# Attention with 64-column matmuls and two quantised convolutions: where the heads' half copies stand in ScalarE's queue, in what pieces an intermediate is read back, and in what order a projection's products are issued

## The chip, the cores and the metric

The kernel runs on one core of one Trainium2 chip. The metric is the device time of one execution in microseconds, as the median of several runs. The profile is that of one execution and is read beside the time of that same execution.

## The reference

There are 16 images of 128 channels and 32 x 32 pixels, in float32. Layer 0 is attention over the 1024 pixels with 4 heads of 128 channels each. Layer 1 is two 3 x 3 convolutions with quantised inputs and weights, each followed by a batch normalisation over all images.

```python
# layer 0
qkv = einsum('bchw,oc->bohw', x, w_qkv) + b_qkv           # 4 heads, q, k, v of 128 channels
scores = einsum('bnc,bcm->bnm', q, k) * c ** (-0.5)
attn = softmax(scores, axis=-1)
out = einsum('bnm,bmc->bnc', attn, v)                      # then heads side by side: 512 channels
x = einsum('bchw,oc->bohw', out, w_out) + b_out + x
# layer 1
identity = x
out = batchnorm(conv3x3(act_quant(x), weight_quant(w1)))   # act_quant: 16 levels in 0..1
out = batchnorm(conv3x3(act_quant(out), weight_quant(w2)))
x = out + identity
```

## The kernel before

**Attention.** The folded weights make one matrix per head out of the query and key weights, and one out of the value and output weights. Steps follow one another in one long list: 64 heads (image by image), four steps k = 0 to 3 per head. A step (`scores`) makes four score tiles of 128 keys by 512 queries. Each tile is a pair of products that write 64 output partitions each, the two *lanes*, and `halves` issues one on each lane. In the instruction stream of TensorE each float32 product stands as two matmuls. ScalarE exponentiates each tile (line 585) out of one of three PSUM banks `pss`, and VectorE forms the three further combinations that a seven-product scheme needs (`mix`, lines 570 to 574). One step later `attend` multiplies them with the turned input in seven products on alternating lanes and adds them up in four PSUM banks, `psa` 0 to 3, over the four steps of the head.

**The end of a head.** After the last `attend` of head g, in step `end`, ScalarE copies the four banks to SBUF. `evacuate` (line 625) takes banks 1 and 3 in the second half of step `end`. `evacuate_rest` (line 630) takes banks 0 and 2 in the next step, each behind one exponential of that step. `combine` then puts the quadrants together in three parts. Part 0 makes three copies between halves of the partitions (lines 641 to 643) and one sum on VectorE (L644). Part 1 copies `s3[BOTTOM]` from `y[TOP]` (L648) and adds (L649). Part 2 copies `sa[BOTTOM]` from `y[BOTTOM]` (L651) and adds twice (L653, L654). So L648 needs the sum L644, L649 needs L648, and L651 needs L649. Meanwhile the exponentials are summed by DMAs that accumulate (L595, issued by POOL, the first by SP). `sum_up` and `normalise` make the inverses, multiply (L721) and, at every second head, `mix` the result `z`.

**The projection.** When an image's four heads are done, `project_out` makes four banks, one at a time, out of `z` and the folded output weights `wb_sb` (L761). In banks 0 and 3 one of the two products has 512 columns and the other has 256, on the other lane. `gather_out` combines the four banks; a first convolution in six row filters follows in later steps (`rows_product`, `rows_output`), and its result is stored to `y1_dram`.

**What sets the order.** The calls are written down with `at(step, half, ...)`: half 0 runs between a step's scores and its attend, half 1 behind the attend. The compiler then orders each engine's queue by itself, earlier calls first among those that it holds ready, so an instruction written later can stand earlier in a queue. `tc.issue_after(ins)` holds an instruction behind another of the same engine. The list `stepped` holds the last step's four exponentials for that purpose. `product` ties TensorE's products into one chain with it; `project_out` does not use it. [...]

**The second convolution.** After the last head, `y1_dram` is read back in three pieces of 2, 3 and 10 images (L1174, queue of SP), and then the residual `res` (L1179). `quantize2` quantises an image: one ScalarE pass (L1189), one VectorE pass (L1190), and one on either engine (L1194 or L1196). Images 3, 5, 7, 9, 11 and 13 are convolved by row filters (`filtered_conv`, tiles `psf`), the others directly (`conv`, L282, tiles `psc`). In program order image 5 is quantised before image 4. At the end each image is scaled, the residual is added, and the result is stored.

Of the kernel before, what the change touches and what calls it, by code (L numbers as in the profile page):

```python
# [193 lines left out]
def fast_path(  # L194
# [18 lines left out]
    B, C, N = x.shape  # L213
# [28 lines left out]
    AWAY = range(0, B - 1)  # L242
    ys = [None if b in AWAY else keep.tile([P, N], F32, name=f"y{b}") for b in range(B)]
    pads = []
    for i in range(NPAD):
        t = padp.tile([P, H + 2, W + 2], BF16, name=f"pad{i}")
# [3 lines left out]
    def quantize(b, src, scale, bias, r0=0, r1=H):  # L250

        cut = slice(r0 * W, r1 * W)
        t = qtp.tile([P, (r1 - r0) * W], F32, tag="qt", name="qt")
        if b == B - 1 and scale == A_LEVELS and r1 == H:
            nc.vector.tensor_scalar(t, src[:, cut], scale, 0.0, ALU.mult, ALU.max)
        else:
            nc.scalar.activation(t, src[:, cut], AF.Relu, bias=bias, scale=scale)
        nc.vector.tensor_scalar(t, t, A_LEVELS, MAGIC, ALU.min, ALU.add)
        into = pads[b % NPAD][:, r0 + 1 : r1 + 1, 1 : W + 1]
        t = t.rearrange("p (h w) -> p h w", w=W)  # L260
        if b == B - 1:
            return nc.vector.tensor_scalar(into, t, MAGIC, FACTOR, ALU.subtract, ALU.mult)
        return nc.vector.tensor_scalar(into, t, MAGIC, None, ALU.subtract)
# [104 lines left out]
    with ExitStack() as ph:  # L368
# [20 lines left out]
        TOP, BOTTOM = slice(0, PH), slice(PH, P)  # L389
        LANES = (TOP, BOTTOM)  # L390
        NK = NCH // 2
        xt, us, xts, es, sides, avs, psa, accs, evs = {}, {}, {}, {}, {}, {}, {}, {}, {}
        zs, pjs, vlast = {}, {}, []
        exps, sums_added, attended, quantized, pe = [], [], [], [], []
        stepped = []
# [4 lines left out]
        def product(out_, lhsT, rhs, start=True, stop=True):  # L400

            with tc.issue_after(pe[0]) if pe else nullcontext():
                done = nc.tensor.matmul(out_, lhsT=lhsT, rhs=rhs, start=start, stop=stop)  # L403
            pe[:] = [done.ins]
            return done
# [50 lines left out]
        wb_sb = once.tile([P, 7, 2, PH], F32, name="wb_sb")  # L456
# [164 lines left out]

        def evacuate(g):
            evs[g] = [evp.tile([P, HALF], F32, tag=f"s{i}", name=f"ev_{g}_{i}") for i in range(4)]
            for i in (1, 3):
                nc.scalar.copy(evs[g][i], psa[g][i])  # L625

        def evacuate_rest(g):
            for n, i in enumerate((0, 2)):
                with tc.issue_after(stepped[n]):
                    nc.scalar.copy(evs[g][i], psa[g][i])  # L630
            psa.pop(g)

# [2 lines left out]
        def combine(g, part):  # L637
            sa, sb, s3, sd = evs[g]
            if part == 0:
                y = avs[g, "y"] = evp.tile([P, HALF], F32, tag="y", name=f"y_{g}")  # L640
                nc.scalar.copy(y[TOP], s3[BOTTOM])
                nc.scalar.copy(y[BOTTOM], sd[TOP])
                nc.scalar.copy(sd[TOP], sd[BOTTOM])
                nc.vector.tensor_tensor(y, sa, y, ALU.add)  # L644
                return
            y = avs[g, "y"]
            if part == 1:
                nc.scalar.copy(s3[BOTTOM], y[TOP])  # L648
                nc.vector.tensor_tensor(y, y, s3, ALU.add)  # L649
            elif part == 2:  # L650
                nc.scalar.copy(sa[BOTTOM], y[BOTTOM])  # L651
                avs[g] = avp.tile([P, N], F32, tag="av", name=f"av_{g}")
                nc.vector.tensor_tensor(avs[g][:, HALF:], y, sd, ALU.add)  # L653
                nc.vector.tensor_tensor(avs[g][:, 0:HALF], sa, sb, ALU.add)  # L654
                evs.pop(g), avs.pop((g, "y"))
# [93 lines left out]
        def project_out(b, bank):  # L749


            four = [
                [(0, A11, B11, W0), (1, S3, T3, W1)],
                [(1, A22, T4, W0), (0, A12, B21, W0)],
                [(1, S2, T2, W0), (0, S4, B22, W0)],
                [(1, S1, T1, W0), (0, S3, T3, W2)],
            ]
            ps = ps_m.tile([P, HALF], F32, tag="mm", name=f"pso_{b}_{bank}")
            for pair in range(2):
                for t, weight, head, cut in four[bank]:  # L760
                    nc.tensor.matmul(  # L761
                        ps[LANES[t], cut],
                        wb_sb[:, weight, pair],
                        zs[b, pair][:, head, cut],
                        start=(pair == 0),
                        stop=(pair == 1),
                    )
            if b not in pjs:
                names = ("sa", "sb", "s3", "sd", "y", "s2")
                pjs[b] = [pjp.tile([P, HALF], F32, tag=n, name=f"{n}_{b}") for n in names]  # L770
            sa, sb, s3, sd, y, s2 = pjs[b]
            if bank == 0:
                nc.scalar.copy(sa[TOP], ps[TOP])  # L773
                nc.scalar.copy(y[BOTTOM, W1], ps[BOTTOM, W1])
            elif bank == 1:
                nc.scalar.copy(sb, ps)
            elif bank == 2:
                nc.scalar.copy(s3[TOP], ps[TOP])
                nc.scalar.copy(s2[TOP], ps[BOTTOM])
            else:  # L780
                nc.scalar.copy(sd[BOTTOM], ps[BOTTOM])
                nc.scalar.copy(sd[TOP], ps[BOTTOM])
                nc.scalar.copy(y[BOTTOM, W2], ps[TOP, W2])
# [237 lines left out]
        def at(step, half, fn, *args):  # L1021

            later.setdefault(2 * step + half, []).append((fn, args))
# [8 lines left out]
        for hf in range(NHF):  # L1032
            warm_up(1)
            ps = ps_a.tile([P, HALF], F32, tag=f"a{2 + hf}", name=f"psu_0_{hf}")
# [16 lines left out]
        for g in range(LAST):  # L1051
            b, h = heads[g]

            end = (g + 1) * NK
            at(end + 1, 0, sum_up, g)
            at(end, 1, evacuate, g)
            at(end + 1, 0, evacuate_rest, g)
            at(end + 1, 0, combine, g, 0)
            at(end + 1, 1, combine, g, 1)
            at(end + 2, 0, combine, g, 2)  # L1060
            if b < B - 1:
                at(end + 4 - h % 2, 0, normalise, g)
            elif g < LAST - 1:
                at(end + 3, 0, normalise, g)
            else:
                at(end + 2, 1, normalise, g)
            at(max(g * NK + 1, 2), 0, project_u, g + 1, 0)
            at(max(g * NK + 2, 3), 0, project_u, g + 1, 1)
            if b < B - 1 and h == NH - 1:
                for bank, (step, half) in ((2, (5, 1)), (1, (6, 1)), (3, (7, 0)), (0, (7, 1))):  # L1070
                    at(end + step, half, project_out, b, bank)
                at(end + 8, 0, gather_out, b, 0)
                at(end + 8, 0, gather_out, b, 1)
                at(end + 9, 0, gather_out, b, 2)
            elif b == B - 1 and h < 2:
                for m, (step, half) in enumerate((((4, 1), (5, 1)), ((4, 1), (5, 0)))[h]):
                    at(end + step, half, project_plain, g, m)
            if h == NH - 1:
                at(end + 9, 1, lambda b: quantize(b, accs[b], A_LEVELS, 0.0), b)
                at(end + 10, 0, transform_rows, b)  # L1080
                at(end + 10, 1, sums_range, b)
                for i in range(len(PAIRS)):
                    at(end + 11 + (i + 1) // 2, (i + 1) % 2, rows_product, b, i)
                at(end + 13, 1, rows_output, b)
                at(end + 14, 0, first_statistics, b)
                if b + 2 < B:
                    at(end + 9, 1, load, b + 2, nc.scalar)
            if h == 2 and b + 1 < B:
                at(end - 2, 0, load_turned, b + 1, 0)
                at(end + 3, 1, turned_differences, b + 1, 0)  # L1090
                at(end + 3, 0, load_turned, b + 1, 1)
                at(end + 6, 1, turned_differences, b + 1, 1)
# [4 lines left out]
        for step in range(n_steps):  # L1097
            g, k = divmod(step, NK)
# [38 lines left out]
    with ExitStack() as ph:  # L1137
# [31 lines left out]


        scale1, bias1 = bn_params(0)
        for lo, hi in ((0, 2), (2, 5), (5, len(AWAY))):
            back = resp.tile([P, hi - lo, N], F32, name=f"back{lo}")
            nc.sync.dma_start(out=back, in_=y1d[lo:hi].rearrange("b c n -> c b n"))  # L1174
            for i in range(lo, hi):
                ys[AWAY.start + i] = back[:, i - lo]
# [55 lines left out]
        for r0, r1 in ((0, 10), (10, RPH + 2), (RPH + 2, H)):  # L1232
            first = quantize2(0, r0, r1)
# [23 lines left out]
        for b in range(B):  # L1257
            ends = parts.get(b, (0, N))
            for lo, hi in zip(ends, ends[1:]):
                y = ys[b][:, lo:hi]  # L1260
# [280 lines left out]
```

## Time and profile before

| what | value |
|---|---|
| median of 3 runs | 2025.08 us (2025.01 to 2025.44) |
| the profiled execution | 2024.81 us, span 2023.0 us |
| TensorE matmul / weight load | 1978.9 us (98%) / 967.3 us (48%) |
| VectorE | 1540.6 us (76%) |
| ScalarE | 1179.7 us (58%) |
| GpSimd | 182.6 us (9%) |
| mean granted TensorE clock | 0.992 |

A row of the page's groups reads: line, engine, operation, tile written and tiles read, shape, number; then busy time in us and the mean of one in ns; then the idle time of the engine just before these instructions and what ended most of it. A row of the waits reads: who waited for whom; then the sum in us, how often, and the longest. A row of a timeline reads: start, length, engine, line, operation and tiles, number of merged instructions, and in brackets the idle time before them with what ended it. A row of stretches gives, for each engine, its busy time and number of instructions, then the granted clock, the busy share of the DMA engines and what they moved in GB/s. Names such as `psa` leave out buffer numbers.

### The profile page before, as it was taken

How to read it: one execution, taken by the hardware profiler on the slowest of the kernel's cores; microseconds unless marked ns; L12 is line 12 of the kernel's file. 1: busy time of each engine (PE TensorE's matmuls, PEld its weight loads, DVE VectorE, ACT ScalarE, POOL GpSimd, SP SyncE). 2: the span in 40 equal slices, each digit the busy share in tenths (PEclk: the TensorE clock that was granted, in tenths of full speed). 3: DMA queues.
4: the chain of work that ended last, by engine and by line, in shares of the span. 5: the costliest groups of instructions: out<-in, count | busy, mean ns of one | idle time of the engine just before them, and what ended most of it. 6: DMA issues, size and time to landing. Idle time of an engine off the chain costs nothing.

```text
span 2023.0 us, 26071 instructions
## 1 busy us (share of the span) xinstructions
PE 1978.9 (98%) x9697; PEld 967.3 (48%) x9697; DVE 1540.6 (76%) x2703; ACT 1179.7 (58%) x2028; POOL 182.6 (9%) x218
## 2 busy tenths in 40 slices
PE   9999999999999999999999999999999999999983
PEld 4344544545454454545445454444544445454531
DVE  5786869778686876868787685878768597777887
ACT  4556556555655655565565556556565565656575
POOL 1110010100000000001000000100100000010020
PEclk9999999999999999999999999999999999999997
DMA  4333433433343433434334333433433343332184
GB/s 121 85 84 92 97 70 98 90 87 96 83 102 65 105 84 84 95 82 100 78 96 93 84 94 74 105 83 94 95 79 92 70 110 79 94 89 73 40 325 168
DMA packets 56216, 193.80 MB, mean 96 GB/s; under 512 B 6160, under 2 KB 6544, under 8 KB 56080
## 3 DMA queue, kind: packets, MB, share of 16 engines
q0 software_dynamic: 27216, 99.10, 25.7%
q1 hardware_dynamic: 25744, 83.18, 11.0%
q10 hardware_dynamic: 3120, 9.77, 1.5%
q8 instruction: 78, 1.28, 0.3%
q14 instruction: 58, 0.48, 0.1%
HBM read 35.27 MB, written 24.64 MB: 30 GB/s over the span
## 4 chain that ended last, share of the span: by engine, by line
PE 82%; DVE 12%; issue 3%; ACT 2%; DMA 1%; DVEq 0%; POOL 0%; ACTq 0%; POOLq 0%
PE pss L403 36%; PE psa L403 31%; PE pso L761 5%; PE psu L403 5%; DVE e L571 2%; PE psc L282 2%; PE psw L403 2%; DVE e L574 1%; ACT e L585 1%; DVE z L721 1%; DVE part L661 1%; DVE back L1267 1%; DVE e L570 1%; DVE side L689 1%; PE psf L1214 1%
## 5 line engine op out<-in xcount | busy, mean ns | idle before, releaser
L403 PE MATMUL pss<-u,x 128*64 128x512 f32 (+1 forms) x4128 | 1043.3, 590 | 4.4 <-ACT e L585 2.7
L403 PE MATMUL psa<-e,xt 128*64 128x512 f32 x3472 | 897.5, 592 | 0.0
L585 ACT ACTIVATE e<-pss 128x512 f32<-128x512 f32 x1008 | 591.6, 599 | 383.8 <-PE pss L403 375.9
L403 PEld LDWEIGHTS pss<-u,x 128*64 128x64 f32 x4128 | 430.5, 137 | 458.3 <-issue 346.7
L403 PEld LDWEIGHTS psa<-e,xt 128*64 128x64 f32 x3472 | 375.8, 137 | 377.0 <-issue 302.0
L570 DVE TENSOR_TENSOR e<-e 128x512 f32<-128x512 f32 x252 | 170.7, 678 | 309.9 <-ACT e L585 309.9
L571 DVE TENSOR_TENSOR e<-e 128x1024 f32<-128x1024 f32 x252 | 307.5, 1220 | 18.8 <-ACT e L585 13.7
L595 POOL DMA_DIRECT2D es<-e x189 | 163.0, 863 | 1695.0 <-DVE e L574 1157.2
L574 DVE TENSOR_TENSOR e<-e 128x512 f32<-128x512 f32 x252 | 173.1, 687 | 14.3 <-DVE e L571 0.9
L403 PE MATMUL psu<-x,at_sb 128*64 128x512 f32 x512 | 177.7, 595 | 0.0
L761 PE MATMUL pso<-z,wb_sb 128*64 128x512 f32 (+1 forms) x480 | 134.6, 540 | 0.0
L625 ACT COPY ev<-psa 128x512 f32<-128x512 f32 x126 | 70.8, 587 | 67.3 <-PE psa L403 66.8
L534 ACT ACTIVATE u<-psu,au_sb 128x512 f32<-128x512 f32 x127 | 87.3, 687 | 17.6 <-PE psu L403 15.6
L661 DVE TRANSPOSE_TENSOR_REDUCE part<-es 128x32 f32<-128x1024 f32 (+1 forms) x65 | 79.3, 1220 | 8.3 <-DMA es<-e 8.3
L403 PEld LDWEIGHTS psu<-x,at_sb 128*64 128x64 f32 x512 | 58.7, 138 | 56.4 <-issue 48.6
L648 ACT COPY ev<-y 64x512 f32<-64x512 f32 x63 | 38.9, 617 | 79.3 <-DVE y L644 79.3
L701 DVE STREAM_TRANSPOSE rb<-sums 128x1024 f32<-128x1024 f32 (+1 forms) x66 | 80.0, 1211 | 2.1
L721 DVE TENSOR_TENSOR z<-av,rb 128x512 f32<-128x512 f32 x120 | 78.2, 683 | 0.0
L761 PEld LDWEIGHTS pso<-z,wb_sb 128*64 128x64 f32 x480 | 53.3, 136 | 43.1 <-issue 41.4
L630 ACT COPY ev<-psa 128x512 f32<-128x512 f32 x126 | 72.8, 579 | 0.3 <-PE psa L403 0.3
L651 ACT COPY ev<-y 64x512 f32<-64x512 f32 x63 | 38.8, 616 | 58.7 <-DVE y L649 58.4
L789 DVE TENSOR_TENSOR y<-sa,s 64x512 f32<-64x512 f32 x15 | 10.2, 683 | 66.7 <-ACT sa L773 66.7
(193 smaller groups left out, 1384.7 us busy)
## 6 DMA issues: line engine op xcount, KB each, us to landing
es<-e POOLq DMA_DIRECT2D x189, 512.0 KB, 4.5
es<-e SPq DMA_DIRECT2D x63, 512.0 KB, 2.9
xt<-in_xturned_dram SPq DMA_DIRECT2D x32, 256.0 KB, 3.0
x_dram<-acc SPq DMA_DIRECT2D x16, 512.0 KB, 2.9
x<-in_x_dram ACTq DMA_DIRECT2D x15, 512.0 KB, 4.1
y_dram<-y SPq DMA_DIRECT2D x15, 512.0 KB, 2.6
res<-x_dram SPq DMA_DIRECT2D x1, 7680.0 KB, 38.6
back<-y_dram SPq DMA_DIRECT2D x1, 5120.0 KB, 20.9
```

Of the source, the lines that this page charges most:

```text
L403: done = nc.tensor.matmul(out_, lhsT=lhsT, rhs=rhs, start=start, stop=stop)
L534: copied = nc.scalar.activation(dst, ps, AF.Identity, bias=au_sb[:, h : h + 1])
L570: nc.vector.tensor_tensor(e[:, T3], e[:, B12], e[:, B22], ALU.add)
L571: nc.vector.tensor_tensor(e[:, T1 : T2 + 1 : T2 - T1], e[:, B12 : B11 + 1], e[:, B11 : T3 + 1 : T3 - B11], ALU.subtract)
L574: return nc.vector.tensor_tensor(e[:, T4], e[:, T2], e[:, B21], ALU.add)
L585: exps[:] = [nc.scalar.activation(e[:, 2 * c + 1 - m], ps, AF.Exp).ins]
L595: nc.gpsimd.dma_start(out=sides[g], in_=mine, accum_op=ALU.add)
L630: nc.scalar.copy(evs[g][i], psa[g][i])
L661: nc.vector.tensor_reduce(part, total.rearrange("p (k c) -> p k c", c=Q), AX.X, ALU.add, apply_transpose=True,)
L701: nc.vector.transpose(rb, rinv.unsqueeze(2).to_broadcast([P, n, Q]))
L721: nc.vector.tensor_tensor(z[:, 2 * (h % 2) + 1 - m], av[:, ts(m, HALF)], rb[:, ts(m, HALF)], ALU.mult)
L761: nc.tensor.matmul(ps[LANES[t], cut], wb_sb[:, weight, pair], zs[b, pair][:, head, cut], start=(pair == 0), stop=(pair == 1),)
```

## The change

In `evacuate`, bank 2 is copied along with banks 1 and 3, and only bank 0 is left for `evacuate_rest`, behind the first exponential of the step. Part 1 of `combine` moves from the second half of step `end + 1` to the first half of `end + 2`, where part 2 already is (in the last image it stays), and the two half copies L648 and L651 are held behind the second and the fourth exponential. `normalise` of every second head moves by half a step. `project_out` issues its products through `product`, in an order written out: in banks 1 and 2 as before, in banks 0 and 3 the first, the second, the second and the first again. The read back of 10 images is cut into one of 4 and one of 6.

```diff
         def evacuate(g):
             evs[g] = [...]
-            for i in (1, 3):
+            for i in (1, 3, 2):
                 nc.scalar.copy(evs[g][i], psa[g][i])

         def evacuate_rest(g):
-            for n, i in enumerate((0, 2)):
-                with tc.issue_after(stepped[n]):
-                    nc.scalar.copy(evs[g][i], psa[g][i])
-            psa.pop(g)
+            with tc.issue_after(stepped[0]):
+                nc.scalar.copy(evs[g][0], psa.pop(g)[0])
...
             if part == 1:
-                nc.scalar.copy(s3[BOTTOM], y[TOP])
+                with tc.issue_after(stepped[1]):
+                    nc.scalar.copy(s3[BOTTOM], y[TOP])
                 nc.vector.tensor_tensor(y, y, s3, ALU.add)
             elif part == 2:
-                nc.scalar.copy(sa[BOTTOM], y[BOTTOM])
+                with tc.issue_after(stepped[3]):
+                    nc.scalar.copy(sa[BOTTOM], y[BOTTOM])
...
-            for pair in range(2):
-                for t, weight, head, cut in four[bank]:
-                    nc.tensor.matmul(
-                        ps[LANES[t], cut],
-                        wb_sb[:, weight, pair],
-                        zs[b, pair][:, head, cut],
-                        start=(pair == 0),
-                        stop=(pair == 1),
-                    )
+            first, second = four[bank]
+            order = [(*first, 0), (*second, 0), (*second, 1), (*first, 1)]
+            if bank in (1, 2):
+                order = [(*first, 0), (*second, 0), (*first, 1), (*second, 1)]
+            for t, weight, head, cut, pair in order:
+                product(
+                    ps[LANES[t], cut],
+                    wb_sb[:, weight, pair],
+                    zs[b, pair][:, head, cut],
+                    start=(pair == 0),
+                    stop=(pair == 1),
+                )
...
-            at(end + 1, 1, combine, g, 1)
+            at(*((end + 1, 1) if b == B - 1 else (end + 2, 0)), combine, g, 1)
             at(end + 2, 0, combine, g, 2)
             if b < B - 1:
-                at(end + 4 - h % 2, 0, normalise, g)
+                at(end + 4 - h % 2, h % 2, normalise, g)
...
-        for lo, hi in ((0, 2), (2, 5), (5, len(AWAY))):
+        for lo, hi in ((0, 2), (2, 5), (5, 9), (9, len(AWAY))):
```

## The prediction

> **What bounds the kernel now.** I read the page first, then the waits, then the instruction timelines of one batch and of the second convolution.
>
> ```profile
> span 2023.0 us, 26071 instructions
> ...
> PE 1978.9 (98%) x9697; PEld 967.3 (48%) x9697; DVE 1540.6 (76%) x2703; ACT 1179.7 (58%) x2028; POOL 182.6 (9%) x218
> ...
> PEclk9999999999999999999999999999999999999997
> ```
>
> TensorE is busy nearly to the end at full clock, so only time in which it does less than it could counts. "Busy" hides half of that. In the attention part the products are 64 columns wide and run on two lanes. In the trace's list of matmuls each lane starts one 512-column matmul every 0.43 us, and a moment with one lane idle still reads as busy. So I listed the start of every matmul, took 0.427 us for 512 columns, half for 256, and summed what each lane waited beyond that. From 8 to 1876 us the average of the two lanes is idle 23.2 us, although the union shows only 4.4. Some 18 us of it stands in four places that recur or come once: head 0 of a batch, third step, 5.7 us over 15 batches; head 3, third step, 4.5 us over 14; projection bank 3, 2.5 us over 15 (0.33 us of one lane each); the weight folds and constants of the first batch, about 5, which the change does not touch. The waits name the first two:
>
> ```profile
> ACT ev L648 <- DVE y L644: 79.3, 63, 3.1
> ...
> ACT ev L651 <- DVE y L649: 58.4, 60, 1.6
> ...
> PEld pss L403 <- ACT e L585: 48.0, 112, 1.9
> ```
>
> ScalarE sits in two half copies of `combine` until VectorE has added, and score matmuls wait for exponentials. ScalarE's timeline in head 0 of batch 6 shows the order:
>
> ```profile
> 728.66 0.69 ACT L534 ACTIVATE u<-psu,au_sb 128x512 f32<-128x512 f32 x1
> 731.08 0.62 ACT L648 COPY ev<-y 64x512 f32<-64x512 f32 x1 [1.73 <-DVE y L644]
> 732.48 0.62 ACT L651 COPY ev<-y 64x512 f32<-64x512 f32 x1 [0.78 <-DVE y L649]
> 733.12 1.57 ACT L585 ACTIVATE e<-pss 128x512 f32<-128x512 f32 x3
> ```
>
> The third step's score matmuls start at 730.67; two products take 0.86, so its first exponential could have begun near 731.7. It begins at 733.12, behind both copies. With three score banks the fourth tile needs the first exponential's bank: the lanes stop for 0.29 and 0.53 us at 733.77.
>
> After attention the largest single hole, in TensorE's timeline and ScalarE's:
>
> ```profile
> 1943.23 4.64 ACT L1189 ACTIVATE steps<-back,bias,scale 128x1024 bf16<-128x1024 f32 x4 [2.26 <-DVE half L1228]
> ...
> 1949.65 5.50 PE L282 MATMUL psc<-pad,wq 128*128 128x512 bf16 x18 [7.33 <-DVE pad L1194]
> ```
>
> The releaser "half" ended long before; what really ended is the third read back:
>
> ```profile
> 1921.80 1.65 SPq L1174 DMA_DIRECT2D back<-y_dram  x2
> ...
> back<-y_dram SPq DMA_DIRECT2D x1, 5120.0 KB, 20.9
> ```
>
> Its issue is at 1922.3, plus 20.9 gives 1943.2. Image 5, whose quantising stands first in ScalarE's queue, is in that piece; image 4, which TensorE needs next, arrived in the piece before but queues behind it.
>
> **What the Trainium skill says.** "PSUM — Partial Sum Buffer", Engine vs sequencer instructions: ScalarE's queue is strictly first in, first out. The trace agrees: exponentials at 733.12 follow the copy's end at 733.10. "TensorE: Matmul & The Clock Gate", Part 1: over 3.4 us of idleness halve the clock. It agrees: after the 7.33 us hole 18 matmuls take 5.50 us, against 3.97 in the chain of waits later. "DMA: Bandwidth & Descriptors", Queues, rings and completion order: one queue's descriptors are consumed in ring order. The landings agree roughly: the three pieces and `res` land in the order of issue at 1924.1, 1930.1, 1943.2 and 1962.1.
>
> **The change, part by part.** No matmul, DVE operation or byte is added; one DMA is.
>
> *Combine's copies, a step later.* L648 goes from the half step before the third step's scores to behind their second exponential, L651 behind the fourth. Both still cost 0.62 us, 126 copies in all, in ScalarE time that is 42% idle. The first exponential is then no longer behind a DVE wait. If L648 itself has to wait, exponentials three and four queue behind it; L644 ended at 731.04 in head 0 and at 821.8 in head 3, before the second exponential would end (1.02 us after the scores' start for the first tile, 0.86 for the second, 0.60 of its own: 733.1 and 824.4), so there is nothing to wait for. Behind L651 stand one `u` copy and the next step's exponentials, 3.4 us away. The DVE adds (0.68 us each) follow their copies; `mix` may shift by one add, while the attend that needs it starts 2.4 us after it ended (739.1 against 741.5). Gain: 5.7 + 4.5 = 10.2 us at most, nothing at least. I take 8.5, leaving a sixth for heads where another ScalarE copy comes first.
>
> *Normalise of odd heads half a step later.* Only DVE operations move, no DMA and nothing on POOL or SP. `z` was finished at 739.7 and its projection begins at 754 or later: cost nothing, cover 14 us.
>
> *Evacuation 1, 3, 2 before, only 0 between exponentials.* A third copy of 0.58 us moves ahead of the next step's first exponential, and one of the two in between goes. That work sum is zero. Those places hold two half copies of 0.62 as fillers; if one moves back, the exponential stays at 724.93, where it is. Its latest harmless start: scores begin at 723.18, the fourth tile is needed 2.57 later, less 0.60, so 725.15, a margin of 0.22. Value zero; bounds −1 (a slightly earlier release) and the third rival below.
>
> *Projections' order.* Bank 3 went lane 1 (512), 0 (256), 1 (512), 0 (256):
>
> ```profile
> 772.55 0.59 PE L761 MATMUL pso<-z,wb_sb 128*64 128x256 f32 x2
> 772.87 0.59 PE L403 MATMUL pss<-u,x 128*64 128x512 f32 x1
> 773.30 1.02 PE L761 MATMUL pso<-z,wb_sb 128*64 128x512 f32 x4
> ```
>
> The first narrow pair starts at 772.55 and occupies its lane for 0.43 us; the second could not start before 773.31, since a wide product stood between them. With 1, 0, 0, 1 both narrow products run together. Gain 0.33 / 2 x 15 = 2.5 us. Bank 0 had no gap and needs none; banks 1 and 2 keep their order. Bound below: 0. I take 2.2. The chain that now holds these products in order is the order they had.
>
> *Read back in four.* Images 5 to 8 become a piece of 2.10 MB. From 1930.1 to 1943.2 5.24 MB came, 0.40 MB/us, so they land at 1930.1 + 5.2 = 1935.3, 7.8 us earlier. SP issues one more DMA, some 0.4 us, ahead of `res`, which lands at 1962 and is needed at 1995: nothing. Image 4's quantising then fits into ScalarE's idle 1.3 us gaps of 1935 to 1941, and TensorE could go on at 1942.3: 7.3 us of hole and 1.5 of slow clock, 8.9 at most. VectorE is next:
>
> ```profile
> 1935.00:1943.00 8.00, 7.32 (x34) 2.95 (x31) 4.33 (x8) 2.35 (x4) 2.21 (x2) 1.00 1.03 424
> 1943.00:1949.00 6.00, 0.00 (x0) 0.00 (x0) 5.79 (x9) 4.64 (x4) 2.67 (x2) 0.72 1.01 418
> 1949.00:1955.00 6.00, 5.35 (x19) 2.10 (x20) 4.39 (x8) 4.98 (x6) 2.67 (x2) 0.71 1.03 424
> 1955.00:1992.00 37.00, 37.00 (x178) 17.09 (x176) 33.85 (x58) 24.33 (x32) 6.84 (x6) 1.00 0.19 76
> ```
>
> From 1935 to 1992 its busy column sums to 48.4 us of 57. Eight of idleness can go, and I leave 2 in which it waits for inputs: gain 6.5, bounds 0 (pieces interleave and land together) and 8.9. Images 9 to 14 still land near 1943; ScalarE has 10 us of work before it asks for image 9.
>
> **Sum.** The profiled execution took 2024.8 us, 1.8 more than its span and 0.3 less than the median of the runs. 8.5 + 2.2 + 6.5 = 17.2, so 2007.6, and with the 0.3 about 2008.
>
> **Rivals.**
> Forecast, 0.62: as above, 2003 to 2014 from the bounds.
> *Only the read back and the lanes pay*, 0.19: the bank copies moved ahead of the exponential take what the half copies give back, some 0.15 us a head. 2025.1 − 8.7 = 2016; with the read back alone 2019. For it: the margin of 0.22. Against: filler copies can yield.
> *Slower*, 0.15: at the evacuation ScalarE takes three bank copies and both half copies before the first exponential, which then starts at 725.5. That exponential, its neighbours and bank 0's copy, now behind the first one and possibly behind the third, all come late; the next head's attend, whose first product writes bank 0, starts at 726.6 and would find it copied 0.6 to 1.0 us late. 62 heads x 0.8 = 50, less the 17: about 2058. It decides from 17.2 / 62 = 0.28 us of lane stop per head. Against it: the half copies were put before the exponential only where it was not ready.
> *Nothing moves*, 0.04: the copies stand in the same places in the queue as before and the pieces land together; 2025.
>
> Two tenths of a per cent, 4 us, is about what a measurement of this kernel tells from no change. The first two cases and part of the fourth give faster 0.81, same 0.04, slower 0.15. The range 2002 to 2022 holds the first two cases, some 0.81.
>
> **What would show it.** Right: L648 and L651 between exponentials with hardly any idle before them; the wait of score weight loads for exponentials well under 48 us; no 0.33 us gap between bank 3's narrow products; the hole before the fifth image's convolution (7.33) under 1.5 us and 18 matmuls there in about 4 us. Wrong: an idle time of attend products for L630, first exponentials starting over 1.7 us after their scores, ScalarE still waiting for a read back near the same place, or a new hole at image 9.

## The result and the profile after

The changed kernel takes 2002.36 us (median of 4 runs, 2000.92 to 2002.61) against 2025.05 us before (4 runs, 2024.70 to 2025.44). The ratio is 0.9886, with a 95% interval of 0.9869 to 0.9904. It is faster, by 22.7 us where 17.2 were forecast, and lies just below the 2003 to 2014 that the prediction's bounds gave for its own case. The profiled execution took 2000.92 us, 23.9 less than that of before. It can be cut at the first `psc` matmul of the second convolution, which stands at 1919.5 before and at 1903.5 after. Of the 23.9 us, 15.9 lie ahead of it, in the attention part, and 8.0 behind it.

In the file of the changed kernel the two half copies are L647 and L651, the sum that L651 waits for is L648, `quantize2` is L1192 to L1199, and the read back is L1177. The page's first rows:

```profile
span 1999.1 us, 26134 instructions
...
PE 1966.2 (98%) x9697; PEld 982.7 (49%) x9697; DVE 1536.5 (77%) x2703; ACT 1181.8 (59%) x2028; POOL 182.4 (9%) x218
```

TensorE's share is 98% as before. The share cannot show the gain, because a moment with one idle lane counts as busy. From the waits (who waited for whom, sum in us, times, longest):

```profile
ACT ev L651 <- DVE y L648: 31.5, 17, 2.2
...
PEld pss L403 <- ACT e L585: 22.1, 81, 0.4
...
ACT ev L647 <- DVE y L642: 1.0, 1, 1.0
```

Score weight loads wait 22.1 us for exponentials instead of 48.0, and never longer than 0.4. The copy L647 waits once in the whole kernel. The copy L651 still waits 1.9 to 2.2 us in one head of 15 images, but it stands behind the last exponential of its step, and the lanes do not stop there. ScalarE's timeline in head 0 of batch 6, the place shown before:

```profile
726.20 0.60 ACT L585 ACTIVATE e<-pss 128x512 f32<-128x512 f32 x1 [2.79 <-PE pss L403]
727.06 0.60 ACT L585 ACTIVATE e<-pss 128x512 f32<-128x512 f32 x1 [0.26 <-PE pss L403]
727.68 0.62 ACT L647 COPY ev<-y 64x512 f32<-64x512 f32 x1
728.32 1.09 ACT L585 ACTIVATE e<-pss 128x512 f32<-128x512 f32 x2
729.43 0.62 ACT L651 COPY ev<-y 64x512 f32<-64x512 f32 x1
```

The first exponential now waits for its scores and for nothing else, and both copies run between exponentials without idle time before them. For the read back, SP's queue and then TensorE's timeline:

```profile
1905.85 2.31 SPq L1177 DMA_DIRECT2D back<-y_dram  x3
```

After the first piece three more are issued in a row instead of two. TensorE's work in the second convolution:

```profile
1924.88 1.49 PE L1217 MATMUL psf<-rows,wq 128*128 128x512 bf16 x6
1926.20 4.13 PE L282 MATMUL psc<-pad,wq 128*128 128x512 bf16 x18
...
1934.00 4.13 PE L282 MATMUL psc<-pad,wq 128*128 128x512 bf16 x18 [1.02 <-ACT pad L1199]
...
1941.03 4.13 PE L282 MATMUL psc<-pad,wq 128*128 128x512 bf16 x18 [0.26 <-ACT pad L1199]
```

The hole of 7.33 us is gone: image 4's 18 matmuls follow directly and take 4.13 us. What is left are holes of 1.02 and 0.26 us before images 6 and 8.

The idle time of the two lanes was summed again from the list of matmul starts, as in the prediction, here from 8 us to the first `psc` matmul, in us as the average of the two lanes. The three columns in the middle are experiments described below. Each column is one profiled execution, and an idle time beside a change of step can fall to either side, so a tenth means little:

| place | before | order alone | half copies alone | bank copies alone | after |
|---|---|---|---|---|---|
| head 0, third step | 6.5 | 9.7 | 0.0 | 0.4 | 0.0 |
| head 3, third step | 4.0 | 2.1 | 0.0 | 0.9 | 0.0 |
| projections | 2.9 | 0.2 | 0.5 | 0.8 | 0.0 |
| first image | 6.8 | 6.8 | 5.2 | 6.1 | 5.1 |
| all else | 5.0 | 6.0 | 4.3 | 5.9 | 5.0 |
| sum | 25.2 | 24.7 | 9.9 | 14.1 | 10.1 |

The sum falls by 15.1 us, which is nearly the 15.9 that attention became shorter.

### The profile page after: what moved, and what is told of

Same layout as the page of the kernel before. It is cut to its first block, busy times and chain, and to the rows that moved or that the text cites. A ratio compares the mean times of both kernels' runs of the same rounds, so it can differ in the third digit from the quotient of the medians.

```text
span 1999.1 us, 26134 instructions
## 1 busy us (share of the span) xinstructions
PE 1966.2 (98%) x9697; PEld 982.7 (49%) x9697; DVE 1536.5 (77%) x2703; ACT 1181.8 (59%) x2028; POOL 182.4 (9%) x218
## 4 chain that ended last, share of the span: by engine, by line
PE 97%; DVE 1%; ACT 1%; issue 0%; DVEq 0%; POOL 0%; ACTq 0%; POOLq 0%
PE pss L403 44%; PE psa L403 38%; PE psu L403 6%; PE pso L403 5%; PE psw L403 2%; PE psc L282 2%; DVE back L1270 1%; PE psf L1217 1%; PE unread L403 0%; ACT steps L1192 0%; PE psv L403 0%; ACT back L1267 0%; ACT pad L1199 0%; PE ps_a L403 0%; DVE late L292 0%
## 5 line engine op out<-in xcount | busy, mean ns | idle before, releaser
L403 PE MATMUL pss<-u,x 128*64 128x512 f32 (+1 forms) x4128 | 1032.4, 589 | 0.0
L403 PEld LDWEIGHTS pss<-u,x 128*64 128x64 f32 x4128 | 438.5, 137 | 434.9 <-issue 399.1
L403 PEld LDWEIGHTS psa<-e,xt 128*64 128x64 f32 x3472 | 379.9, 137 | 371.1 <-issue 352.0
L403 PE MATMUL psu<-x,at_sb 128*64 128x512 f32 x512 | 183.4, 592 | 0.0
L625 ACT COPY ev<-psa 128x512 f32<-128x512 f32 x189 | 99.2, 593 | 63.1 <-PE psa L403 61.7
L792 DVE TENSOR_TENSOR y<-sa,s 64x512 f32<-64x512 f32 x15 | 10.2, 683 | 66.4 <-ACT sa L776 66.4
L651 ACT COPY ev<-y 64x512 f32<-64x512 f32 x63 | 38.8, 616 | 32.7 <-DVE y L648 31.5
L403 PE MATMUL psw<-rows,filters 128*64 128x256 bf16 x540 | 57.5, 277 | 0.0
L403 PEld LDWEIGHTS <-filters 128*64 128x64 bf16 x540 | 44.8, 109 | 24.0 <-issue 18.6
```

## The experiments

The theory was that of the prediction: three of the five edits pay, each for a stop of its own. The rivals were that some edit does another's work, and that the three bank copies ahead of the exponential cost something. Where a kernel is described as "before plus" or "changed kernel less", nothing else differs.

### The read back alone

Before plus one line:

```diff
-        for lo, hi in ((0, 2), (2, 5), (5, len(AWAY))):
+        for lo, hi in ((0, 2), (2, 5), (5, 9), (9, len(AWAY))):
```

> The kernel before with the read back in four pieces and nothing else. Theory (the whole hole goes, and the slow clock behind it): 8.0 us less than before, convolution of image 4 starting right behind image 3's. Rival, as predicted (VectorE leaves 2 us): 6.5 us less. Rival (pieces land together): no change, hole of 7 us still there.

Measured: 2017.11 us against 2024.95, ratio 0.9961 (0.9947 to 0.9974), so 7.8 us. Images 5 to 8 landed at 1935.5, where the prediction had 1935.3. TensorE's timeline of this kernel:

```profile
1941.83 4.13 PE L282 MATMUL psc<-pad,wq 128*128 128x512 bf16 x18
...
1949.63 4.13 PE L282 MATMUL psc<-pad,wq 128*128 128x512 bf16 x18 [1.02 <-ACT pad L1196]
```

The hole before image 4 is gone and 1.02 us comes back one image later, as in the changed kernel. This edit is separate from the others.

### Images 4 and 5 quantised in the order of need, three pieces kept

```diff
-            if b + 2 < B and b + 2 not in FILTERED:
+            if b + 2 < B and b + 2 not in FILTERED and b != 2:
                 quantize2(b + 2)
+            if b == 1:
+                quantize2(4)
```

> The kernel before with three pieces as they were, but image 4 quantised before image 5 in program order. Theory (half of the hole is queue order: image 4 was there since 1930 and only stood behind image 5; image 5 still lands at 1943 and its row filters are ready 5 us later): convolution of image 4 follows without a hole, a new one of 2 to 3 us stands before image 5's, 4 to 6 us less than before. Rival (only the landing counts): no change, the same hole of 7 us one image later.

Measured: 2021.22 us against 2025.33, ratio 0.9980 (0.9971 to 0.9988), so 4.1 us:

```profile
1941.94 4.13 PE L282 MATMUL psc<-pad,wq 128*128 128x512 bf16 x18
...
1952.20 4.13 PE L282 MATMUL psc<-pad,wq 128*128 128x512 bf16 x18 [1.40 <-ACT pad L1196]
```

Image 4 never needed the big piece; it only queued behind image 5. With the order alone its hole goes too, but image 5 itself still waits for 5.24 MB, and holes of 1.29, 0.45 and 1.40 us follow. So the smaller piece is worth 7.8 us, and the order of the queue with the big piece about half of that.

### The projections' order alone

Before plus the new `project_out`.

> The kernel before with the projection's products chained in the written order and nothing else. Theory (one narrow product no longer waits for a wide one on the other lane): 2.5 to 2.9 us less, lane gaps at the projections gone. Rival (the gap is only moved to the next product of the lane): no change, another gap of 0.3 us behind bank 3.

Measured: 2024.34 us against 2024.95, ratio 0.9993 (0.9985 to 1.0001): not told apart from nothing. The theory fell. The gaps of the projections are gone (2.9 to 0.2 in the table), but head 0's third step took some 3 us more (6.5 to 9.7), while head 3's took 1.9 less. The waits of this kernel show that the cause of these stops is still there:

```profile
ACT ev L648 <- DVE y L644: 76.3, 49, 3.0
...
PEld pss L403 <- ACT e L585: 45.2, 115, 2.1
```

In most images the list of starts shows an exchange: one lane no longer loses 0.33 us at bank 3, and in the next head 0 the two lanes stop for 0.29 and 0.75 us instead of 0.29 and 0.53. In two images the stops there are longer, of 1.0 and 1.5 and of 1.3 and 1.8 us, which makes up over half of the 3 us. The profiled execution was the slowest of the 13 (2025.47), and three others took 2022.0 to 2022.6. Whether these had no such long stops is not shown.

### The half copies alone

```diff
             if part == 1:
-                nc.scalar.copy(s3[BOTTOM], y[TOP])
+                with tc.issue_after(stepped[1]):
+                    nc.scalar.copy(s3[BOTTOM], y[TOP])
...
             elif part == 2:
-                nc.scalar.copy(sa[BOTTOM], y[BOTTOM])
+                with tc.issue_after(stepped[3]):
+                    nc.scalar.copy(sa[BOTTOM], y[BOTTOM])
...
-            at(end + 1, 1, combine, g, 1)
+            at(*((end + 1, 1) if b == B - 1 else (end + 2, 0)), combine, g, 1)
```

> The kernel before with the two half copies (L648, L651) moved alone; evacuation 1, 3 then 0, 2 and normalise stay. Theory (the half copies ahead of the first exponential are the whole cause): 12 us less, as with all the head parts together. Rival (bank 2's copy between the exponentials delays the sum that L648 waits for, so that the third exponential waits behind it): 4 to 8 us less, with idle time of ScalarE before L648.

Measured: 2010.61 us against 2024.95, ratio 0.9925 (0.9912 to 0.9939), so 14.3 us, more than the 12 of the theory. Both third steps stand at zero in the table, and the projections fell to 0.5 although their order is the old one. TensorE's timeline at a third bank shows why:

```profile
762.69 4.00 PE L403 MATMUL pss<-u,x 128*64 128x512 f32 x16
766.13 1.42 PE L763 MATMUL pso<-z,wb_sb 128*64 128x256 f32 x6
```

Four narrow matmuls and two wide ones stand merged in one row. By the list of starts the narrow ones begin at 766.13, 766.34, 766.56 and 766.80, without the gap of 0.33 us, and the first wide one at 766.53. So the narrow lane is 0.40 us ahead here, where it was 0.76 ahead in the kernel before (772.55 and 773.30). In both kernels, and in all 15 images, the second narrow pair begins just behind the first wide matmul and never ahead of it. As a narrow pair takes 0.43 us, a lead of 0.76 leaves a gap of 0.33, and a lead of 0.40 leaves none.

The lead goes with the stops. Here a gap is left in the first image alone (0.28 us), where some stops remain. In the kernel with the bank copies alone, described below, gaps of 0.31 to 0.37 us stand in four images of 15: in the first, and in three that follow a stop of 0.3 us or more; the other eleven have no stop of over 0.1 us ahead of them. That it is the unevenness of a stop that puts one lane ahead is inferred: the two lanes stop for 0.29 and 0.53 us in head 0 of the kernel before, which is 0.24 of the 0.35 us between the two leads, but the trace does not name the lanes.

In the profiled execution attention ended 16.1 us earlier, but 2.0 of that was lost behind it, 1.5 of them in one place:

```profile
1933.56 7.00 PE L282 MATMUL psc<-pad,wq 128*128 128x512 bf16 x18 [7.33 <-DVE pad L1196]
```

The hole is the same 7.33 us, but the matmuls after it take 7.00 us and not 5.50. The stretches of this kernel (length; busy time and number for TensorE, its weight loads, VectorE, ScalarE, GpSimd; then clock, DMA share, GB/s) show the clock still at half from 1936 to 1938 and for a part of the next 2 us:

```profile
1936.00:1938.00 2.00, 2.00 (x6) 0.73 (x5) 1.56 (x2) 1.58 (x3) 1.82 (x2) 0.50 1.03 424
1938.00:1940.00 2.00, 2.00 (x8) 0.69 (x6) 1.23 (x3) 2.00 (x3) 0.00 (x0) 0.62 1.03 426
1940.00:1942.00 2.00, 2.00 (x11) 0.89 (x10) 0.71 (x2) 1.76 (x4) 0.00 (x0) 1.00 1.01 418
```

By the starts of the matmuls it was back at full 6.0 us after 1933.56. In the kernel before it was back 2.9 us after the hole's end at 1949.65:

```profile
1952.50:1954.50 2.00, 2.00 (x10) 0.88 (x9) 1.56 (x3) 2.00 (x3) 1.42 (x2) 1.00 1.03 424
```

### All the head edits

Half copies, bank copies and `normalise` together, with old projections and three pieces.

> The kernel before with everything that concerns the heads (evacuation 1, 3, 2 then 0; half copies behind the second and fourth exponential a step later; normalise of odd heads half a step later), without the projection's order and the read back. Theory (lane waits for exponentials go whole, the small ones behind them too): 12 to 13 us less, and the three single parts add up to the 22.7 of the whole change. Rival, as predicted (a sixth stays): 8.5 us less; then the parts would not add up, and some 5 us came from their acting together.

Measured: 2009.70 us against 2024.95, ratio 0.9923 (0.9910 to 0.9937), so 15.3 us. Next to the half copies alone (14.3, intervals overlapping) the other head edits add nothing that can be told. Attention ends at 1903.4 in both.

### The changed kernel less the new order

> The changed kernel with the projection's old products (no chain, both pairs in the same order). Theory (bank 3's gap was the offset between two lanes that the heads' uneven stops had left; without those stops the lanes run in step): within 0.7 us of the changed kernel, gaps at the projections under 0.6 us in all 15 images. Rival, as predicted (the order of a wide and a narrow product makes the gap): 2.2 to 2.9 us more than the changed kernel, 0.33 us in each image.

Measured: 2001.54 us, ratio 0.9882 (0.9867 to 0.9898), against 0.9886 for the changed kernel. The order is worth nothing that can be told there either: with the stops gone there is a gap in the first image alone for it to close.

### The changed kernel less the half copies

L648 and L651 back at their old place.

> The changed kernel with the two half copies back where they stood (a half step earlier, behind no exponential); banks 1, 3, 2, normalise, projection order and read back stay. Theory (these two copies are nearly all of the heads' gain): 13 to 15 us more than the changed kernel, with a lane wait of some 9 us in the third step of head 0. Rival (copying bank 2 early brings the sums forward, so that the copies no longer wait): 3 us or less more.

Measured: 2005.69 us against 2025.33, ratio 0.9903 (0.9888 to 0.9918), only some 3.3 us over the changed kernel, a quarter of what the half copies gain by themselves. The theory (13 to 15) fell. So another of the edits does nearly the same work; the next kernel has it alone.

### The bank copies alone

```diff
-            for i in (1, 3):
+            for i in (1, 3, 2):
...
-            for n, i in enumerate((0, 2)):
-                with tc.issue_after(stepped[n]):
-                    nc.scalar.copy(evs[g][i], psa[g][i])
-            psa.pop(g)
+            with tc.issue_after(stepped[0]):
+                nc.scalar.copy(evs[g][0], psa.pop(g)[0])
```

> The kernel before with the bank copies alone changed: 1, 3 and 2 together, 0 behind the first exponential; the half copies, normalise, projections and read back are as before. Theory: copying bank 2 one step-half earlier by itself lets the part-0 copies and VectorE's sum end about 8 us sooner, so that both half copies are done before the third step's scores need the exponential. Then it gains nearly what all four head edits gained without the half copies (about 11 to 12 us): 2013 to 2014.5, and TensorE's wait of score weights for exponentials falls from 48 to about 25 us. Rival: it needs normalise's later half-step to get the sum early; then it gains under 5 us, over 2020. Second rival: with the three bank copies ahead of the exponential and the half copies there too it is slower than 2025.

Measured: 2013.20 us against 2024.98, ratio 0.9941 (0.9928 to 0.9955), so 11.8 us, as the theory said. ScalarE's timeline in head 0 of batch 6, then the sum of part 0 on VectorE, then a row of the waits (line numbers two lower: the half copies are L646 and L649):

```profile
724.35 0.62 ACT L646 COPY ev<-y 64x512 f32<-64x512 f32 x1
726.45 0.61 ACT L649 COPY ev<-y 64x512 f32<-64x512 f32 x1 [1.48 <-DVE y L647]
727.12 0.60 ACT L585 ACTIVATE e<-pss 128x512 f32<-128x512 f32 x1
```

```profile
722.87 0.68 DVE L642 TENSOR_TENSOR y<-ev,y 128x512 f32<-128x512 f32 x1
```

```profile
PEld pss L403 <- ACT e L585: 24.7, 78, 1.3
```

Both half copies still stand ahead of the exponential, and the second still waits, but both are done in time. Counted from the first exponential of the step before (719.91 here, 724.93 before), the sum starts 3.0 us later here and 5.4 later in the kernel before: bank 2 is copied sooner, so is what is copied out of it, and VectorE takes the sum 2.5 us sooner in its queue. The expectation's "8 us" compared absolute times of two executions and was wrong by the 5 us that this kernel had gained up to there. Against the half copies, 4 us of lane time are left: in heads of batch 15 and in head 3 of batches 10 and 12, where the copies are late all the same, and in the first image.

### The changed kernel less the bank copies

> The changed kernel with the old bank copies (1 and 3 together, 0 and 2 behind the first and second exponential). Theory: bank copies and half copies remove the same wait, so with the half copies moved this is worth nothing: 2001 to 2003, within 1 us of the changed kernel. Rival: bank 2's earlier copy has a share of its own (attend of the next head finds its bank earlier): 2 to 4 us slower, and TensorE's attend products wait for the copy.

Measured: 2000.82 us, ratio 0.9879 (0.9863 to 0.9894). Beside the half copies the bank copies are worth nothing that can be told; the median is 1.5 us below that of the changed kernel, and the ranges of the runs overlap.

### The changed kernel less the move of normalise

> The changed kernel with normalise of every second head at its old half step. Theory: z is finished some 14 us before its projection in either place, so nothing: within 0.7 us of the changed kernel at about 2002. Rival: normalise in the old place stands in VectorE's queue ahead of a sum or a mix that the next attend needs: 2 us or more slower, with attend products waiting for mix.

Measured: 2001.83 us, ratio 0.9884 (0.9869 to 0.9899). Worth nothing that can be told, as predicted.

### Two edits of five

Before plus the half copies' move and the four pieces.

> Two of the five edits: the half copies behind the second and fourth exponential, and the read back in four pieces. Bank copies, normalise and the projections' order are as before. Theory: gains of the two add, 14.3 and 7.8 us, so 2003.0 (2002 to 2004), within 1.5 us of the changed kernel at 2002. Rival: bank copies, normalise and order together are worth over 3 us beside them: over 2005.

Measured: 2001.55 us against 2024.98, ratio 0.9882 (0.9867 to 0.9898), so 23.4 us: all of the changed kernel's gain. Its wait of score weight loads is that of the changed kernel too:

```profile
PEld pss L403 <- ACT e L585: 21.6, 81, 0.4
```

This kernel and the three that take away the order, the bank copies or `normalise` lie between 2000.8 and 2001.8. None can be told from the changed kernel, so no better version was shown, only simpler ones.

### The predicted slower case, brought about

The changed kernel with the three half copies of part 0 written at the evacuation, so that they stand ahead of the next step's exponentials. Part 0 keeps its sum alone:

```diff
         def evacuate(g):
...
             for i in (1, 3, 2):
                 nc.scalar.copy(evs[g][i], psa[g][i])
+            sa, sb, s3, sd = evs[g]
+            y = avs[g, "y"] = evp.tile([P, HALF], F32, tag="y", name=f"y_{g}")
+            nc.scalar.copy(y[TOP], s3[BOTTOM])
+            nc.scalar.copy(y[BOTTOM], sd[TOP])
+            nc.scalar.copy(sd[TOP], sd[BOTTOM])
```

> The changed kernel with the three half copies of combine's first part written in front of the step's scores, so that three bank copies and two or three half copies stand before its first exponential, and bank 0's copy behind the third. Nothing is added. This is the rival that the prediction priced. Theory (the fourth score tile and the first attend product stop the lanes once the exponential is later than 1.97 us after its scores): 0.8 to 1.7 us in each of 62 heads, 50 to 105 us more than the changed kernel. Rival (three banks of scores and a later catch-up swallow it): under 10 us more.

Measured: 2045.39 us against 2025.33, ratio 1.0099 (1.0083 to 1.0114). That is 43.0 us over the changed kernel, or 0.69 for each of 62 heads. ScalarE's timeline and the waits:

```profile
733.64 0.62 ACT L629 COPY y<-ev 64x512 f32<-64x512 f32 x1
734.29 0.62 ACT L628 COPY y<-ev 64x512 f32<-64x512 f32 x1
734.81 0.61 ACT L630 COPY ev<-ev 64x512 f32<-64x512 f32 x1
735.33 1.54 ACT L585 ACTIVATE e<-pss 128x512 f32<-128x512 f32 x3
```

```profile
PEld pss L403 <- ACT e L585: 84.9, 126, 1.3
...
PEld psa L403 <- ACT ev L634: 26.0, 62, 2.6
```

Three copies ahead of the exponential make three exponentials late at once, and the copy of bank 0 (L634) behind them holds up the next head's attend, 62 times. The mechanism of that rival is real. In the changed kernel the compiler's order let only one of the part-0 copies stand ahead of the exponential (at 718.34 in the head shown above, the exponential at 718.99), and the lanes do not stop for that.

## Why the prediction was right or wrong

**The reading of the bound was right.** The lanes' idle time at the two third steps, 10.5 us over 15 images, vanished to the last tenth, and the hole of 7.33 us did too. The signs that the prediction named are all there: copies between exponentials, the wait of weight loads at 22.1 us, no gap at bank 3, 18 matmuls in about 4 us and no hole above 1.5. Only L651 waits longer than "hardly any idle before" it, without harm.

**The term for the half copies was mis-sized: 8.5 taken, 15.6 measured, over its own bound of 10.2.** This is the step of the prediction that failed most. The clean measure is the step from four pieces alone (2017.11) to two edits (2001.55), in which no hole blurs the end of attention. Three parts were short. "Leaving a sixth for heads where another ScalarE copy comes first" held back 1.7 us; no row of the profile showed such a head, and there was none. The projections' gaps were put down to another cause, and went with the stops (2.4 us by the table). And the first image was said to be untouched by the change; it gained 1.6 us. With the 10.5 at the two third steps these make 14.5; the remaining 1.1 us the table leaves open, though "all else" fell by 0.7 with the half copies alone.

**The term for the projections' order failed: 2.2 taken, 0 measured**, alone and in the changed kernel. The sentence "the second could not start before 773.31, since a wide product stood between them" read the trace rightly: with the old order the second narrow pair waits for the first wide matmul to begin in every image. The step that failed is the next one, "0.33 / 2 x 15". It took the gap for a loss that the order makes by itself and that can be had in full. But how long the gap is depends on how far one lane is ahead, 0.76 us before and 0.40 without the stops. A repair at the gap lengthened the next stop of one lane by 0.22 us in most images, and a repair of the stops removed the gap in all images but the first. Why the second narrow pair waits for the first wide matmul, and the first pair does not, stays open.

**The term for the read back was a little small: 6.5 taken, 7.8 alone and 8.0 behind the cut in the changed kernel.** The landing was hit within 0.2 us. Its "1.5 of slow clock" set 5.50 us of one view against 3.97 of another; in the timelines it is 5.50 against 4.13, so 1.4. Too much was kept back for VectorE: "Eight of idleness can go, and I leave 2" took its busy sum of 48.4 us as fixed. The stretches of before, and of after 15.9 us earlier and 8.0 shorter, have the columns given above:

```profile
1935.00:1992.00 57.00, 49.67 (x229) 22.14 (x226) 48.37 (x81) 36.30 (x45) 14.39 (x12) 0.94 0.48 197
```

```profile
1919.10:1968.10 49.00, 47.72 (x222) 21.30 (x221) 46.11 (x81) 35.29 (x43) 14.19 (x12) 1.00 0.56 229
```

VectorE's idle time fell from 8.6 to 2.9 us, about as the prediction had it, but with the same 81 pieces of work its busy time fell by 2.3 too. A busy sum can hold waiting. The timeline of before, both engines:

```profile
1946.18 2.67 POOL L1205 TENSOR_TENSOR rows<-padf 128x544 bf16<-128x544 bf16 x2 [7.11 <-DVE padf L1194]
...
1947.78 1.35 DVE L1190 TENSOR_SCALAR steps<-steps 128x1024 bf16<-128x1024 bf16 x1
```

This pass over `steps`, 0.41 us elsewhere, takes 1.35 and ends at 1949.13, just behind the second of GpSimd's row sums, which began at 1947.52 and ended at 1948.85. Two more, at 1953.37 and 1964.97, take 0.83 and 1.29 us and end 0.3 us behind a row sum that had begun before them. The Trainium skill, "SBUF — State Buffer", Who interferes with whom, says that a VectorE instruction in a two-port mode, which `tensor_scalar` can enter, and a GpSimd instruction exclude each other for the whole instruction. The trace agrees with it here. In the changed kernel no pass begins in the middle of a row sum, none takes over 0.43 us, and the twelve of the stretch fell from 7.0 to 4.8 us. That they no longer meet was luck of the new order in time and not foreseen. They are not the whole account: VectorE's own ten row sums rose from 7.0 to 8.2 us in the same stretches, and where the rest of the 2.3 comes from was not broken down.

**Bank copies at zero: right in the sum, wrong in the reason.** "That work sum is zero" counted ScalarE's copies and not what hangs on them: bank 2 sooner is a sum on VectorE sooner. Alone the edit is worth 11.8 us. It and the half copies' move are two ways of removing one wait, so 14.3 and 11.8 alone make 15.3 together.

**Normalise at zero** was right. **The slower rival** was priced well, at 0.8 us a head where 0.7 were measured once its condition was made. Its condition did not come about. As the prediction said against another rival, "filler copies can yield": two of part 0's three copies stand between the exponentials.

## What to carry to other kernels

Where two lanes or queues share an engine, measure the idle time of each from the starts and not the engine's busy share, and look for an uneven stop ahead of a gap before repairing the gap itself. A wait of B for a chain A can be taken away by moving B back or by starting A sooner; price both, and do not add them. And a term held back "for safety" needs a row of the profile as much as a term that is claimed.

## What the runs showed of the hardware that was not expected

- **Products overtake one another between column lanes.** In the kernel with the order alone the products of the third bank are chained as wide, narrow, narrow, wide, each as two matmuls. By the trace's starts the four narrow ones began at 771.62, 771.84, 772.06 and 772.27, the first two wide ones, which stand ahead of them, at 772.38 and 772.81. In the kernel with the half copies alone they are written as wide, narrow, wide, narrow without a chain. There the narrow ones began at 766.13, 766.34, 766.56 and 766.80, the wide ones at 766.53, 766.96, 767.39 and 767.82. If the queue keeps the written order, the last narrow one began ahead of three wide ones that stand earlier.
- **The price of one and the same hole varies.** Behind 7.33 us of idleness, 18 matmuls took 5.50, 5.55, 5.77, 6.58 and 7.00 us in five kernels, against 4.13 without a hole, as the half clock lasted 2.9, 3.0, 3.4, 5.1 and 6.0 us. The Trainium skill, "TensorE: Matmul & The Clock Gate", Part 1, says that the clock's window runs freely, so that the moment of the change depends on where in it the first matmul falls. These numbers agree with that, but the 0.5 us either way that the page gives for it is too small here. An edit upstream can gain or lose 1.5 us by it, which has nothing to do with the edit.
- **A lead of one lane lasts.** In the kernel with the bank copies alone the lanes stopped for 0.37 and 0.89 us at 1291.8, and 67 us later, at that image's bank 3, the second narrow pair waited 0.37 us. A stop of 0.34 us of one lane at 1528.2 was followed, again 67 us later, by a gap of 0.31. The eleven images without such a stop ahead of them have no gap.
